# A decoder block: cross-attention's division moves to VectorE's block transposes, three norms share a tile, and the work is put in a new order

## The chip, the cores and the metric

The kernel runs on one core of a Trainium2 chip. The metric is the device time of one execution in microseconds, lower is better. Engines are named as in the profile: PE is TensorE's matrix products, PEld its weight loads, DVE is VectorE, ACT is ScalarE, POOL is GpSimd, SP is SyncE, which only issues transfers here.

## What is computed

One pre-norm decoder block in float32 on `x` of 32 sequences, 128 tokens, 256 features, with a context of the same shape:

```python
x = x + linear_attention(layernorm(x))     # 16 heads of 16; q, k = elu(.)+1; causal by cumulative sums;
                                           # num / (den + 1e-6), then an output projection; biases
x = x + cross_attention(layernorm(x), ctx) # 16 heads of 16; softmax(q k / 4) v; no biases, no projection
x = x + ffn(layernorm(x))                  # silu(x W1 s1) * (x W2 s2), gelu(. H1 s), gelu(. H2 s), . W3 s
```

The feed-forward width is 1024 and its weights are ternary with a scale for each output. The kernel uses a cheaper product for them, which is exact only if the weights survive a cast; it therefore compares each loaded weight with its original ("tests" below) and has a full-precision branch for the case that one differs. The branch is not taken with these inputs.

## The kernel before

**Pairs and steps.** The attention works on 16 pairs of sequences. A pair goes first through the units whose names begin with `a_` (self-attention), and three steps later (`SKEW`) through the `b_` units (cross-attention). A step `m` gives the engines the `a_` units of pairs near `m` and the `b_` units of pairs near `m - 3`. Each unit is a generator, cut by `yield` into parts; a part mostly holds the instructions of one engine. The lists `head`, `first0` to `first2`, `both`, `close`, `begins`, `alone`, `last` and `rest` are the order, written out: each entry advances one unit by one part. `both` is used for the steps 3 to 14, the steady ones; `close` is step 15, `begins` step 16, `alone` 17, `last` 18, `rest` 19. Inside an engine, instructions run strictly in this order.

**Self-attention of a pair.** `a_norm` takes statistics on VectorE (`pair_stats`, lines 129 to 151) and an inverse square root by three Newton rounds, on GpSimd from the third pair on, then GpSimd writes the normed rows. `a_transpose` turns them on TensorE, ScalarE copies. `a_keys`, `a_queries`, `a_values` project (`pp`, `pv`, lines 364, 372). `a_scores` puts all heads of one sequence into two double banks of PSUM (`sa`), and VectorE multiplies by the causal mask into `at` (line 488), for which there is one buffer per half. `a_weighted` multiplies with the values and a column of ones that gives the denominators (`pf`, line 409), in a layout with features on partitions. VectorE then transposes 32 by 32 blocks out of PSUM (`fa`, line 505), adds a constant and takes reciprocals, GpSimd multiplies (`oa`), VectorE transposes back (`oT`, line 517). `a_out` projects (`pw`) and VectorE adds to `x` (line 525).

**Cross-attention of a pair.** `b_norm`, `b_transpose`, `b_queries`, `b_keys`, `b_values` are alike. `b_maxima` computes scores once (`sm`) for their row maxima: two reductions on VectorE (line 581) and two small operations; `b_turn_maxima` transposes them (`pz`) and VectorE spreads them (`mT`, line 594). `b_scores` computes scores again (`se`) and adds the negative maxima by one more product (line 606), ScalarE takes exponentials (line 617). `b_weighted` is the same product `pf`, which ScalarE copies (`fb`, line 624). `b_divide` makes four transposes of 128 by 128 on TensorE (`po`, line 630), VectorE takes reciprocals and divides (lines 634, 636), GpSimd adds to `x` (line 643). `b_end` takes the norm of the finished pair for the feed-forward part.

**Buffers.** `sa`, `sm` and `se` share two double banks; every other product takes one of four banks in turn. So a product waits until the reader of the product four before it is done, and scores wait until the scores before them have been read.

**Tests.** `w_test` loads one slice of the weights W1, W2, H1 per step on GpSimd's queue, loads it again in two pieces on SyncE's, and VectorE compares (line 124). The slices of H2 and W3 are loaded and tested in the feed-forward part, in `layer`, two slices per layer from the second block on, until there are none left.

**Feed-forward part.** Eight blocks of four sequences, each value as a high and a low part: GpSimd casts the high one, VectorE subtracts for the low one, and TensorE multiplies both (`ph`, line 220). `beside` and `settle` in the last steps put the first block's input, gates and first products among the last cross-attention units; their low parts are on GpSimd.

The weights of the attention are permuted on the host (`by_group`) to fit the order of heads in `pf`.

## Time and profile before

| | us |
|---|---|
| median of 3 runs | 1106.37 |
| all runs | 1106.37, 1106.64, 1102.03 |
| the profiled execution | 1102.84 |
| its span in the trace | 1101.0 |
| granted TensorE clock, mean | 0.998 of full speed |

The profile's page has the busy time of each engine, the span in 40 slices of 27.5 us with the busy tenths of each engine, the chain that ended last, and groups of instructions: line, engine, operation, output and inputs, count, then busy time and mean ns of one, then the idle time just before them and what ended it. In the order of time, each line is a start, a length, an engine, a line and an operation; a bracket at its end is idle time before it and the releaser. The chain that ended last is 94% TensorE.

### The profile page before, as it was taken

The page shows a single profiled execution, that of the slowest core. Times are in us where ns is not written, and L with a number is a line of the kernel's source. Part 1 is how long each engine was busy: PE and PEld are TensorE (multiplying, and loading weights), DVE is VectorE, ACT ScalarE, POOL GpSimd, SP SyncE. Part 2 cuts the span into 40 slices and gives each one's busy share as a digit, 9 for nine tenths or more (in the row PEclk, how much of TensorE's full clock was granted, in tenths as well). Part 3 has the DMA queues.
Part 4 walks back from the last instruction along what each step waited for, and adds up shares of the span by engine and source line. Part 5 has one row for each costly group of instructions (what it writes and reads, how often), then busy time and mean ns, then how long its engine had stood idle before and what let it go on. Part 6 is the DMA issues. An engine that isn't in the chain of part 4 may idle for free.

```text
span 1101.0 us, 19995 instructions
## 1 busy us (share of the span) xinstructions
PE 1081.7 (98%) x8054; PEld 877.7 (80%) x8054; DVE 601.1 (55%) x1328; ACT 383.4 (35%) x591; POOL 453.3 (41%) x1057
## 2 busy tenths in 40 slices
PE   8989999999999999999999999999999999999997
PEld 6767777777777767688888888888888888888886
DVE  6889999999899876522532533422422422422412
ACT  4234444444444458831311312322312322312221
POOL 4656666666666455561411412312312312312311
PEclk9999999999999999999999999999999999999999
DMA  8001111111111100060110110000000000000000
GB/s 283 1 28 52 49 49 49 61 58 49 50 49 50 30 11 1 2 191 1 39 39 20 39 39 25 24 10 10 20 10 15 6 1 17 4 1 20 1 1 22
DMA packets 26546, 39.25 MB, mean 36 GB/s; under 512 B 2512, under 2 KB 18640, under 8 KB 26448
## 3 DMA queue, kind: packets, MB, share of 16 engines
q1 hardware_dynamic: 22000, 26.09, 7.0%
q0 software_dynamic: 4032, 11.54, 3.3%
q8 instruction: 65, 1.06, 0.4%
q10 hardware_dynamic: 416, 0.28, 0.1%
q14 instruction: 33, 0.27, 0.1%
HBM read 33.71 MB, written 4.19 MB: 34 GB/s over the span
## 4 chain that ended last, share of the span: by engine, by line
PE 94%; DVE 2%; ACT 1%; POOL 1%; issue 0%; DMA 0%; SPq 0%; DVEq 0%
PE ph L220 52%; PE pp L364 10%; PE py L864 6%; PE pf L409 5%; PE pv L372 5%; PE sa L393 3%; PE se L393 3%; PE sm L393 3%; PE pw L372 3%; PE po L630 1%; PE pt L353 1%; PE se L606 1%; DVE nm L581 1%; PE pt L209 1%; DVE at L488 1%; PE pz L591 1%
## 5 line engine op out<-in xcount | busy, mean ns | idle before, releaser
L183 DVE TENSOR_TENSOR gl<-hg,gh 128x512 fp32r<-128x512 f32 x126 | 87.6, 695 | 344.1 <-POOL gh L182 341.2
L182 POOL CAST gh<-hg 128x512 fp32r<-128x512 f32 x128 | 79.1, 618 | 358.9 <-ACT hg L244 358.9
L244 ACT ACTIVATE hg<-ph,col 128x512 f32<-128x512 f32 x128 | 88.3, 690 | 364.7 <-PE ph L220 364.6
L220 PE MATMUL ph<-sl,H 128*128 128x512 f32 x512 | 199.3, 389 | 0.5 <-POOL sl L183 0.5
L220 PE MATMUL ph<-sh,H 128*128 128x512 f32 x512 | 199.5, 390 | 0.0
L220 PE MATMUL ph<-gh,H 128*128 128x512 f32 x512 | 199.2, 389 | 0.0
L220 PE MATMUL ph<-gl,H 128*128 128x512 f32 x512 | 199.2, 389 | 0.0
L220 PEld LDWEIGHTS ph<-sl,H 128*128 128x128 f32 x512 | 96.1, 188 | 20.8 <-POOL sl L183 0.9
L220 PEld LDWEIGHTS ph<-sh,H 128*128 128x128 f32 x512 | 96.1, 188 | 20.4 <-issue 0.3
L220 PEld LDWEIGHTS ph<-gl,H 128*128 128x128 f32 x512 | 96.1, 188 | 20.0
L220 PEld LDWEIGHTS ph<-gh,H 128*128 128x128 f32 x512 | 96.1, 188 | 19.9
L220 PE MATMUL ph<-xh,W 128*128 128x512 f32 x256 | 101.4, 396 | 0.1
L220 PE MATMUL ph<-xl,W 128*128 128x512 f32 x256 | 100.7, 393 | 0.2 <-DVE xl L183 0.2
L182 POOL CAST sh<-hs 128x512 fp32r<-128x512 f32 x64 | 58.5, 915 | 71.8 <-DVE hs L236 71.7
L581 DVE TENSOR_REDUCE nm<-sm 128x8 f32<-128x1024 f32 x64 | 75.2, 1215 | 17.9 <-PE sm L393 17.9
L488 DVE TENSOR_TENSOR at<-sa,causal 128x1024 f32<-128x1024 f32 x64 | 75.2, 1216 | 8.7 <-PE sa L393 5.5
L617 ACT ACTIVATE pr<-se 128x1024 f32<-128x1024 f32 x64 | 62.0, 1020 | 27.6 <-PE se L606 27.6
L236 DVE SCALAR_TENSOR_TENSOR hs<-ph,col,sil 128x512 f32<-128x512 f32 x64 | 48.0, 750 | 41.9 <-PE ph L220 22.4
L234 ACT ACTIVATE sil<-ph,col 128x512 f32<-128x512 f32 x64 | 44.1, 690 | 75.8 <-PE ph L220 75.7
L364 PE MATMUL pp<-xTa,WA 128*128 128x256 f32 x256 | 62.1, 386 | 0.7 <-ACT xTa L356 0.7
L864 PE MATMUL py<-W,gh 128*128 128x256 f32 x256 | 62.7, 285 | 0.0
L864 PE MATMUL py<-W,gl 128*128 128x256 f32 x256 | 62.0, 283 | 0.0
(129 smaller groups left out, 1834.6 us busy)
## 6 DMA issues: line engine op xcount, KB each, us to landing
x<-in_x_dram SPq DMA_DIRECT2D x16, 256.0 KB, 5.5
cT<-in_ctxT_dram SPq DMA_DIRECT2D x16, 256.0 KB, 2.6
stage<-in_h1T_dram SPq DMA_DIRECT2D x16, 256.0 KB, 2.8
H<-in_h1T_dram POOLq DMA_DIRECT2D x8, 512.0 KB, 3.6
H<-in_h2T_dram POOLq DMA_DIRECT2D x8, 512.0 KB, 6.5
out_dram<-y SPq DMA_DIRECT2D x32, 128.0 KB, 1.7
raw<-in_h2T_dram SPq DMA_DIRECT2D x16, 256.0 KB, 2.6
WA<-in_wattn_dram SPq DMA_DIRECT2D x4, 256.0 KB, 4.8
```

Source lines behind the costliest of these rows:

```text
L182: (high_engine.copy if high_engine is nc.scalar else high_engine.tensor_copy)(high, t)
L183: lows.append(lambda: low_engine.tensor_tensor(low, t, high.bitcast(F32), ALU.subtract))
L220: nc.tensor.matmul(pp, lhsT=w[:, k, ts(c, P)], rhs=parts[p], start=(k == 0 and p == 0), stop=(k == len(src) - 1 and p == 1),)
L244: nc.scalar.activation(t, pp, AF.Gelu, scale=col[:, c_scale + c : c_scale + c + 1])
L364: nc.tensor.matmul(pp[:, c, :], lhsT=w[:, d, ts(c, P)], rhs=src[:, d, :], start=(d == 0), stop=(d == DC - 1))
L372: nc.tensor.matmul(pp, lhsT=src[:, d, :], rhs=w[:, d, :], start=(d == 0), stop=(d == DC - 1))
L393: nc.tensor.matmul(sc[g // 2][:, g % 2, 2 * c : 2 * c + 2, :], lhsT=loaded[32 * g : 32 * g + 32, c, ts(j, S)], rhs=streamed[32 * g : 32 * ...
L409: nc.tensor.matmul(pf[32 * g : 32 * g + 32, i, :], lhsT=v[:, 4 * i + g, :], rhs=weights[g // 2][:, g % 2, i, :], start=True, stop=True,)
L488: nc.vector.tensor_tensor(at.rearrange("p g i s -> p (g i) s"), sc[u].rearrange("p g i s -> p (g i) s"), causal.unsqueeze(1).to_broadcast( ...
L581: nc.vector.tensor_reduce(nm[:, 2 * u : 2 * u + 2, :], sc[u], AX.X, ALU.max, negate=True)
L617: nc.scalar.activation(pr, sc[u], AF.Exp)
L864: nc.tensor.matmul(py[:, :D], lhsT=h[k][p][:, ts(j, S)], rhs=W3[:, k, :], start=(k == 0 and p == 0), stop=(k == HC - 1 and p == 1),)
```

## The change

- `a_weighted`'s way from `pf` to divided values is made a function, `divided`, which `b_weighted` now uses too, without the added constant. `b_divide` goes; `b_out` turns the divided values by two transposes of 128 by 128 on TensorE (`pot`), ScalarE copies 256 columns, GpSimd adds to `x`.
- `pf` is filled with the heads in another order, so that the permutation on the host goes.
- `norms(k)` takes the statistics of three pairs (for self-attention `k + 2`, for cross-attention `k - 1`, for the feed-forward part `k - 4`) into one tile, and makes one round of small operations and one Newton iteration on six columns. Only the first two pairs of self-attention have a norm of their own, on VectorE, where a fused operation takes the place of two.
- `w_load` loads the slices of W1, W2 and H1 at the same rate as before but does not test them. `layer` tests all 28 slices, two per layer, from the first block's second layer to the last block's first.
- The lists have a new order. In a steady step TensorE's units were `sm pf pp sa po pp pp pz pf se mT pv pw pf sm pt po pv sa pz pp pt se mT pf pw`; they become `pt sm pt pv pot sa pz pp pw se mT pp sm pf pf sa pz pp pp se mT pv pf pf pot pw`.

```diff
+    means = tiny.tile([P, STEPS, 6], F32, name="means")
+    devs = tiny.tile([P, STEPS, 6], F32, name="devs")
...
+    def deviations(mv, nmean, rstd, engine=nc.gpsimd):
+        wide = [P, mv.shape[1]]
         nc.vector.tensor_scalar(nmean, mv[:, :, 0], -1.0, None, ALU.mult)
...
         for _ in range(NEWTON):
             engine.tensor_tensor(t, rstd, rstd, ALU.mult)
             engine.tensor_tensor(t, t, hv, ALU.mult)
-            engine.tensor_scalar(t, t, 1.5, None, ALU.add)
-            engine.tensor_tensor(rstd, rstd, t, ALU.mult)
+            if engine is nc.vector:
+                engine.scalar_tensor_tensor(rstd, t, 1.5, rstd, ALU.add, ALU.mult)
+            else:
+                engine.tensor_scalar(t, t, 1.5, None, ALU.add)
+                engine.tensor_tensor(rstd, rstd, t, ALU.mult)
...
-                        lhsT=v[:, 4 * i + g, :],
+                        lhsT=v[:, 8 * (i // 2) + 2 * g + i % 2, :],
...
+        def divided(pf, add, tags):
+            f = buffer([P, 4, S], F32, tag=tags[0], name=tags[0], bufs=2 if add else 1)
+            nc.vector.transpose(f.rearrange("p i s -> p (i s)"), pf.rearrange("p i s -> p (i s)"))
+            f = f.rearrange("p i (b w) -> p b i w", w=VW)
+            rden = small.tile([P, 4, 4], F32, tag="rden", name="rden", bufs=2)
+            if add:
+                nc.vector.tensor_scalar(rden, f[:, :, :, HD], add, None, ALU.add)
+                nc.vector.reciprocal(rden, rden)
+            else:
+                nc.vector.reciprocal(rden, f[:, :, :, HD])
+            yield
+            o = buffer([P, 4, 4, HD], F32, tag=tags[1], name=tags[1], bufs=2 if add else 1)
+            nc.gpsimd.tensor_tensor(
+                o, f[:, :, :, 0:HD], rden.unsqueeze(3).to_broadcast([P, 4, 4, HD]), ALU.mult
             )
+            yield
+            oT = buffer([P, DC, S], F32, tag=tags[2], name=tags[2], bufs=2 if add else 1)
+            nc.vector.transpose(
+                oT.rearrange("p c (b q) -> p b c q", q=32), o.rearrange("p b (c e) d -> p b c (e d)", e=2)
+            )
+            return oT
...
+        def norms(k):
+            a, b, e = ((n, 0 <= n < NPAIR) for n in (k + 2, k - 1, k - SKEW - 1))
+            mv = small.tile([P, 6, 2], F32, tag="mv", name="mv", bufs=2)
+            for c, (n, there) in enumerate((a, b, e)):
+                if there:
+                    pair_stats(mv[:, 2 * c : 2 * c + 2], n)
+                if c < 2:
+                    yield
+            of = [c for c, (_, there) in enumerate((a, b, e)) if there]
+            cols = slice(2 * of[0], 2 * of[-1] + 2)
+            yield from deviations(mv[:, cols], means[:, k, cols], devs[:, k, cols])
+            for c, (n, there) in enumerate((a, b)):
+                yield
+                if there:
+                    scal = means[:, k, 2 * c : 2 * c + 2], devs[:, k, 2 * c : 2 * c + 2]
+                    (A, Bs)[c][n]["xn"] = normed_pair(n, *scal, ("xna", "xnb")[c])
...
         def b_weighted(m, j):
             pf = weighted(Bs[m].pop(("w", j)), Bs[m]["v"][:, j])
             yield
-            f = buffer([P, 4, S], F32, tag="fb", name="fb")
-            nc.scalar.copy(f, pf)
-            Bs[m]["f", j] = f
-
-        def b_divide(m, j):
-            f, po = Bs[m].pop(("f", j)), bank("po")
-            for i in range(4):
-                nc.tensor.transpose(po[:, i, :], f[:, i, :], ident)
...
+            Bs[m]["oT", j] = yield from divided(pf, None, ("fb", "ob", "oTb"))
+
+        def b_out(m, j):
+            pt = bank("pot").rearrange("p a s -> p (a s)")[:, : DC * S]
+            oT = Bs[m].pop(("oT", j))
+            for c in range(DC):
+                nc.tensor.transpose(pt[:, ts(c, P)], oT[:, c, :], ident)
+            yield
+            o = buffer([P, D], F32, tag="oc", name="oc", bufs=1)
+            nc.scalar.copy(o, pt)
             yield
             nc.gpsimd.tensor_tensor(xs[m][:, j, :], xs[m][:, j, :], o, ALU.add)
...
-        def w_test(m):
-            if m < prologue or not spare:
-                return
-            n = spare.pop(0)
-            dst = (W1, W2, H1)[FFN_SLICES[n][0]]
-            load(n, dst)
-            pieces = again(lambda: stages.tile([P, TB], F32, tag="stage", name="stage"), n)
-            yield
-            test(dst, *pieces)
+        def w_load(m):
+            if m >= prologue and spare:
+                n = spare.pop(0)
+                load(n, (W1, W2, H1)[FFN_SLICES[n][0]])
+            return
+            yield
...
         both = [
...
+            (a_out, -1, 1), (b_scores, 0, 0), (b_queries, 1), (b_maxima, 0, 1), (norms, 0),
+            (b_weighted, 0, 0), (b_out, -1, 1), (b_queries, 1), (norms, 0), (b_maxima, 0, 1),
+            (a_keys, 1), (b_load, 2), (a_weighted, 0, 0), (a_scores, 0, 1), (b_turn_maxima, 0, 1),
+            (a_bias, 1), (norms, 0), (norms, 0), (b_weighted, 0, 0), (a_scores, 0, 1),
...
         rest = [
...
+            (b_weighted, -1, 1), (b_weighted, -1, 1), (norms, 0), (b_weighted, -1, 1), (norms, 0),
+            (b_weighted, -1, 1), settle, (b_out, -1, 1), (b_out, -1, 1), beside, (b_out, -1, 1), settle,
+            (norms, 0), (norms, 0), (norms, 0), (norms, 0),
...
-        loading, testing = iter(late), iter(late)
+        loading, testing = iter(late), iter(range(len(FFN_SLICES)))
...
-                if blk and c % 4 == 0:
+                if (blk or w is H2) and c % 4 == 0:
                     n = next(testing, None)
-                    waiting = None if n is None else (last_weights(n), *again(raw, n))
+                    waiting = None if n is None else (weights(n), *again(raw, n))
```

## The prediction

> **What bounds the kernel now.** I read the page first, for the busy shares and the forty slices, then the windows by stage, the order of time on TensorE, the waits and the groups.
>
> ```profile
> PE 1081.7 (98%) x8054; PEld 877.7 (80%) x8054; DVE 601.1 (55%) x1328; ACT 383.4 (35%) x591; POOL 453.3 (41%) x1057
> PE   8989999999999999999999999999999999999997
> DVE  6889999999899876522532533422422422422412
> ```
>
> TensorE is full nearly throughout; VectorE is nearly as full, but only in the first 400 us, the attention. The windows separate the stages:
>
> ```profile
> 0.00:50.00 50.00, 44.08 (x364) 34.61 (x364) 39.45 (x111) 16.94 (x38) 28.03 (x78) 1.00 0.46 156
> 100.00:150.00 50.00, 50.00 (x588) 38.67 (x584) 45.76 (x111) 22.26 (x40) 32.82 (x96) 1.00 0.17 54
> 400.00:450.00 50.00, 48.38 (x441) 35.26 (x433) 30.27 (x66) 39.77 (x52) 28.23 (x71) 0.97 0.00 1
> 800.00:900.00 100.00, 100.00 (x477) 84.25 (x476) 32.28 (x59) 23.99 (x34) 23.47 (x33) 1.00 0.03 9
> ```
>
> Columns: stretch, length, busy time of PE, PEld, DVE, ACT, POOL, granted clock, DMA. In the steady steps TensorE has no gap and VectorE works 46 of 50 us; in the feed-forward part VectorE works a third of the time. So a TensorE microsecond saved counts in full, and a VectorE microsecond counts only where its order makes TensorE wait. In the order of time the step repeats every 26.14 us (scores for the maxima start at 73.34, 99.48, 125.62). A piece of one step, and three waits of TensorE outside the steady steps:
>
> ```profile
> 99.41 1.15 PE L393 MATMUL sm<-kb,qb 32*128 32x256 f32 x16
> 103.42 1.15 PE L393 MATMUL sa<-qa,ka 32*128 32x256 f32 x16
> 104.49 0.66 PE L630 MATMUL po<-ident,fb 128*128 128x128 f32 x4
> ...
> 55.92 0.41 PE L409 MATMUL pf<-at,va 128*32 128x128 f32 x4 [1.41 <-DVE at L488]
> ...
> 61.75 1.13 PE L372 MATMUL pw<-WA,oT 128*128 128x256 f32 x4 [1.80 <-DVE oT L517]
> ...
> 468.02 0.66 PE L630 MATMUL po<-ident,fb 128*128 128x128 f32 x4 [0.71 <-ACT fb L624]
> ```
>
> **TensorE in a steady step.** I price a unit by the distance from its start to the next start, since busy times overlap: a projection 1.73, scores 1.07, weighting `pf` 1.01, four transposes 0.44 to 0.50, values 1.73, output projection `pw` 0.86, the `mT` addition 0.52 after 0.78 of scores, and about 0.2 more when an untiled product is followed by a tiled one. Two `po` per step (0.50 and 0.44) become two `pot` of half as many transposes (0.22 and, before scores, about 0.37): 0.35 less. The new order has six tiled runs per step, as before, but weighting and scores alternate in two places instead of four; the new sequence (names of the tiles) is pt 0.53, sm 1.08, pt 0.49, pv 1.73, pot 0.37, sa 1.08, pz 0.16, pp 1.73, pw 0.95, se 0.78, mT 0.52, pp 1.93, sm 1.07, pf 1.01, pf 1.01, sa 1.08, pz 0.16, pp 1.73, pp 1.93, se 0.78, mT 0.52, pv 1.84, pf 1.01, pf 1.01, pot 0.22, pw 0.86: 25.58 us, 0.56 less than 26.14.
>
> Against it stands one new wait. Between the second maxima scores and the next causal scores there were 4.01 us (99.41 to 103.42); the new order puts only two weightings there, 3.09. The two reductions start 1.18 after the scores and take 2.36, so the second half of the banks is free at 3.54 and wanted at 3.36: 0.2 to 0.3 us per step. The other places fit: causal scores after the first maxima come at 3.6, the output transposes of `pot` find their bank free with about 0.2 to spare (keys' three ScalarE copies, 1.75, just end), and values find theirs with 0.5. Taken: 25.58 + 0.25 = 25.83, 0.3 less, over 11 full steps 3.3 us. Bounds: 0.56 a step if the wait is hidden (6.2 us), and plus 0.5 a step if VectorE is 0.8 late (loss 5.5).
>
> **VectorE, ScalarE, GpSimd in the step.** Per batch, VectorE loses the divide (0.29 + 0.34 start to start, line 634, 636) and gains a transpose from PSUM with its reciprocal and one of 256 columns:
>
> ```profile
> L505 DVE STREAM_TRANSPOSE fa<-pf 128x512 f32<-128x512 f32 x32 | 22.8, 713 | 7.7 <-PE pf L409 6.6
> L517 DVE STREAM_TRANSPOSE oT<-oa 128x256 f32<-128x256 f32 x32 | 14.0, 437 | 0.5 <-POOL oa L512 0.5
> L624 ACT COPY fb<-pf 128x512 f32<-128x512 f32 x32 | 18.7, 584 | 50.4 <-PE pf L409 50.4
> L630 PE MATMUL po<-ident,fb 128*128 128x128 f32 x128 | 20.1, 279 | 0.8 <-ACT fb L624 0.7
> ```
>
> That is 0.95 + 0.36 - 0.63 = 0.7 more, 1.4 per step. Three norms in one tile save two of three groups of small operations, 1.0 per step; the moved tests (line 124, two of 0.69 and the reads) save 1.3. VectorE falls from 23.8 to about 23 of 25.8. GpSimd gains two products of 0.65 and loses 24 of 36 Newton operations at 0.28 start to start: 5.4 less. ScalarE copies 256 columns for 512. All are off the path, covered by TensorE. What is queued behind the one risky place: the norm statistics (3.5) and the four small operations (0.5) stand on VectorE directly before the second maxima; laid end to end behind the causal mask they finish at 12.52 where the scores are ready at 12.53. No margin: each 0.1 us of lateness is 0.1 per step.
>
> The Trainium skill speaks against the new transposes: "VectorE: DVE Perf Modes", Rules for kernel authors, gives a 128 by 128 transpose to TensorE when the result may lie in PSUM, and the VectorE one only 32 by 32 blocks; by it nothing would be taken off TensorE and this term would be zero. The trace already has block transposes at 713 and 437 ns with a weighting layout that makes the blocks suffice, on the engine that is not the bound, so the rows decide.
>
> **The prologue.** TensorE's waits between 16 and 62.8 us add up to 2.04 + 0.49 + 0.18 + 0.35 + 0.27 + 1.41 + 0.63 + 1.80 = 7.17. The last three come from two weightings in a row that share the one buffer of masked scores, and an output projection right behind. The new order puts the scores, the cross queries and the next queries between those weightings. Laid out with the rows' durations, the first 2.04 stays (the chain of keys through ScalarE and VectorE is the same), and some 0.3, 0.55, 0.6, 0.1 and 0.5 remain or arise in the first two steps: 4.1 in all, with steady steps beginning near 59. Newton with a fused add and multiply spares three VectorE operations of 0.2 in the first norm, at most 0.4 of the 0.68 wait at 10.1. Taken: 3.5 saved; bounds 4.7 (the most the layout gives) and 0 (new waits as long as the old).
>
> **The end of attention (376 to 472 us).** Ten `po` fewer by half: 2.2 saved. Before, the feed-forward input's transposes wait on GpSimd for 1.2 us in four pieces at 403 to 405 and the low part's split follows at once; between 406 and 412 the granted clock reads 0.80, 0.50 and 0.84 in stretches of 2 us, 1.7 us of work lost. In the new order scores, keys, maxima and transposes stand between that input and the first gates. I count 2 of these 2.9 as saved. Against that: for the last batch the weighting is followed at once by `pot`, with VectorE transpose and reciprocal (1.0), GpSimd product (0.65), VectorE transpose (0.45) and their hand-overs in between, 2.4 us where 0.71 stood: 1.7 lost. A transpose put before the `mT` product in the last steps, and close's causal mask between two scores with 2.3 us where 3.5 are needed, cost about 1.3 together. Sum: 1.2 saved; bounds 5 saved, 3 lost. On the clock, "TensorE: Matmul & The Clock Gate", Part 1, ties the half rate to an idle window of about 3.4 us; the trace halves it after four gaps below 0.6, and keeps 1.00 through the 2.04 gap at 16.7, so the page decides nothing here.
>
> **The feed-forward part.** 24 tests (24 of 0.69 + 0.08, 18.5 us of VectorE) move here; two pieces per four chunks behind the low part, on an engine a third busy, while TensorE runs 14.8 us of products per four chunks. Their loads go through SyncE's queue behind the outputs of the block before, and their tiles are the ones the gates have freed. Cost taken 0; if a gate had to wait for a test, 1.5 us in each of six blocks more, 9 at the worst. The weights' own loads stay on GpSimd, 0.6 each. In the attention SyncE's queue loses the tests' 24 loads; the context loads left in it wait for TensorE to free their buffer, so that brings nothing.
>
> **Sum.** 3.3 + 3.5 + 1.2 = 8.0 off the profiled execution's 1102.84 (span 1101.0): 1094.8. The runs before were 1102.03, 1106.37 and 1106.64, so the profiled one is low by up to 3.8; I put the forecast at half of that above the sum, 1096.5.
>
> **Rivals.** (1) *The saved TensorE time is spent at new waits*: the 0.25 per step is 0.55, the prologue gives 1.5 and the end nothing; 1.5 to 3 saved, about 1100.5 to 1103. For it: VectorE's missing margin; against it: VectorE's load falls. (2) *Slower: VectorE's in-order queue decides the step.* If statistics that wait for GpSimd's sum (cross-attention's last result, now behind a copy) start over 0.55 late, the maxima reductions behind them slip, the causal scores with them, and the saving of 0.56 is used up. At 1.4 late in each of 12 steps: 0.85 x 12 = 10 lost, less 3.5 + 1.2 elsewhere, 5.5 slower, about 1108 to 1112. The sum they wait for is done some 6 us earlier by the layout, which speaks against it. (3) *More than counted*: the 0.25 is hidden and the prologue gives 4.7, the end 2: 12.9 saved, 1090 to 1092. (4) That the change doesn't do what it says: the transposes' end is modelled, and halving them may free nothing; then 0.35 of each step is missing, which is rival 1.
>
> **Chances.** Forecast 0.60, rival 1 with 4 0.20, rival 2 0.10, rival 3 0.10. A measurement of this kernel can tell about 0.5%, 5.5 us, from no change. The forecast's own spread leaves 0.08 of its 0.60 within that; with rival 3, faster is 0.62, within 0.28, slower 0.10. The range 1089 to 1104 takes in the forecast's bounds, rival 3 and most of rival 1; rival 2 is left out.
>
> **What would show it.** Right: steps of 25.7 to 26.0 us; about 0.2 us waits of causal scores on the maxima reduction (line 608 after); steady steps from 58 to 60; full clock around 400; feed-forward stretches still at 100.00. Wrong: steps of 26.1 or longer, waits of tiled scores above 0.5, TensorE gaps in the feed-forward part that end with a test.

## The result and the profile after

The changed kernel takes 1097.41 us (median of six runs, 1096.79 to 1098.78) against 1105.33 for the kernel before (six runs, 1102.03 to 1106.64): ratio 0.9934, 95% interval 0.9918 to 0.995. The profiled execution took 1097.11, its span is 1095.1, so 5.9 less than the span of 1101.0 before. The forecast was 1096.5.

The page first: busy times of the engines, and two rows of the 40 slices.

```profile
PE 1079.6 (99%) x7990; PEld 877.8 (80%) x7990; DVE 610.5 (56%) x1250; ACT 374.8 (34%) x591; POOL 413.8 (38%) x777
PE   8999999999999999899999999999999999999997
DVE  5888888888888877623433433433433432423412
```

TensorE has 64 products fewer; it is still the full engine. VectorE is busier by 9 us in all, GpSimd 40 us less busy. The windows of the changed kernel, with the columns as before:

```profile
0.00:50.00 50.00, 44.82 (x357) 35.09 (x358) 35.59 (x98) 16.34 (x37) 26.39 (x67) 0.97 0.43 146
100.00:150.00 50.00, 50.00 (x552) 38.48 (x547) 44.27 (x93) 22.86 (x42) 25.88 (x56) 1.00 0.12 33
400.00:450.00 50.00, 48.78 (x480) 35.84 (x478) 33.94 (x68) 45.07 (x58) 27.90 (x54) 1.00 0.02 7
800.00:900.00 100.00, 100.00 (x477) 84.33 (x476) 37.03 (x71) 23.65 (x33) 23.67 (x33) 1.00 0.09 30
```

The clock is 0.97 in the first window (it was 1.00) and 1.00 around 400 (it was 0.97). VectorE's tests show in the last row, 37 us for 32, beside a TensorE that has no gap. In the order of time on TensorE a steady step now looks so, from the first to the second causal scores and on to the next second maxima:

```profile
90.28 1.15 PE L402 MATMUL sa<-qa,ka 32*128 32x256 f32 x16
91.36 0.33 PE L618 MATMUL pz<-ident,z 128*128 128x128 f32 x1
...
97.44 1.30 PE L402 MATMUL sm<-kb,qb 32*128 32x256 f32 x16
98.67 1.08 PE L418 MATMUL pf<-pr,vb 128*32 128x128 f32 x32
99.57 1.06 PE L418 MATMUL pf<-at,va 128*32 128x128 f32 x32
100.55 1.83 PE L402 MATMUL sa<-qa,ka 32*128 32x256 f32 x16
102.31 0.33 PE L618 MATMUL pz<-ident,z 128*128 128x128 f32 x1
...
123.58 1.30 PE L402 MATMUL sm<-kb,qb 32*128 32x256 f32 x16
```

From 97.44 to 123.58 is 26.14 us, to the hundredth what a step took before. The same 16 products of causal scores take 1.08 to the next start at 90.28, and 1.76 at 100.55. No bracket on these lines shows the wait, because it lies inside the group. The weight loads (PEld) of the same products show it: the first four are loaded, then the engine stands 0.40 until a maxima reduction (`nm`) is done, then come the other twelve.

```profile
100.55 0.30 PEld L402 LDWEIGHTS sa<-qa,ka 32*128 32x128 f32 x4 [0.20 <-issue]
101.25 0.73 PEld L402 LDWEIGHTS sa<-qa,ka 32*128 32x128 f32 x12 [0.40 <-DVE nm L608]
```

On VectorE at that place:

```profile
98.25 0.18 DVE L150 TENSOR_SCALAR devs<-v 128x6 int32<-128x6 int32 x1
98.35 0.60 DVE L152 TENSOR_SCALAR hv<-v 128x6 f32<-128x6 f32 x1
98.85 2.34 DVE L608 TENSOR_REDUCE nm<-sm 128x8 f32<-128x1024 f32 x2
```

The reductions that free the banks start 1.41 after their scores, where they start 1.18 after them when VectorE is free (112.81 to 113.99 in the same step), and they end at 101.19.

So where did 5.9 us go? The first steady product (`pt` now, `sm` before) starts at 60.14 instead of 62.81: 2.7 saved. The scores for the maxima of step 15 start at 373.56 instead of 376.11: 2.55, so the twelve steady steps gave nothing. The last turn of cross-attention starts at 462.07 instead of 468.02: 5.95, so the end of attention gave 3.4. From there to the end it is 633.0 in both. The end of attention and its waits, in the order of time:

```profile
375.06 0.41 PE L657 MATMUL pot<-ident,oTb 128*128 128x128 f32 x2 [0.35 <-DVE oTb L450]
391.50 0.92 PE L402 MATMUL se<-qb,kb 32*128 32x256 f32 x10 [0.16 <-DVE at L541]
442.77 0.33 PE L618 MATMUL pz<-ident,z 128*128 128x128 f32 x1 [1.03 <-DVE hs L245]
462.07 0.44 PE L657 MATMUL pot<-ident,oTb 128*128 128x128 f32 x2 [2.30 <-DVE oTb L450]
```

These are 3.8 us of waits, against 3.5 before in other places. What the stage saved is busy time of TensorE, 88.16 to 84.49 in the windows between the two marks. Of that, 1.7 is what a lowered clock had taken at 406 to 412. Run 1 below, which gives each turn four transposes again, is only 0.73 longer in this stage (378.24 to 467.48), so the halved turns are worth 0.7 here. About 1 us of the 3.4 is not assigned to a cause.

### The profile page after: what moved, and what is told of

It reads as the page before. It is cut to its first block, busy times and chain, and to the rows that moved or that the text cites. A ratio compares the mean times of both kernels' runs of the same rounds, so it can differ in the third digit from the quotient of the medians.

```text
span 1095.1 us, 19472 instructions
## 1 busy us (share of the span) xinstructions
PE 1079.6 (99%) x7990; PEld 877.8 (80%) x7990; DVE 610.5 (56%) x1250; ACT 374.8 (34%) x591; POOL 413.8 (38%) x777
## 4 chain that ended last, share of the span: by engine, by line
PE 94%; DVE 3%; POOL 2%; issue 1%; ACT 0%; POOLq 0%; DVEq 0%
PE ph L229 52%; PE pp L373 10%; PE py L882 6%; PE pf L418 5%; PE pv L381 5%; PE sa L402 4%; PE sm L402 3%; PE se L402 3%; PE pw L381 2%; PE pt L362 1%; DVE at L541 1%; PE pot L657 1%; PE se L633 1%; PE pz L618 1%; PE pt L218 1%
## 5 line engine op out<-in xcount | busy, mean ns | idle before, releaser
L500 ACT ACTIVATE e<-pp,col 128x256 f32<-128x256 f32 x64 | 26.8, 470 | 127.4 <-PE pp L373 96.7
```

## The experiments

I held four questions open. Do the halved turns count in full? What sets the step at 26.14: the second causal scores' wait (A), or VectorE's load (B)? What did the tests and the order bring? And where does the lowered clock come from, which stood at 406 us in the trace before and stands at 20 us now? Ratios are to the kernel before.

**1. Four turns instead of two.** `b_out` makes the two transposes twice, the second pair beside the first and unread.

```diff
...
-            for c in range(DC):
-                nc.tensor.transpose(pt[:, ts(c, P)], oT[:, c, :], ident)
+            for c in range(2 * DC):
+                nc.tensor.transpose(pt[:, ts(c, P)], oT[:, c % DC, :], ident)
...
```

> The kernel after, with the two transposes of the divided values made twice on TensorE (the second pair is written beside the first and never read), so that TensorE again makes four per batch. Theory A (TensorE's sequence sets the step, plus one wait of the causal scores for the second maxima reduction, 0.68 us a step of which 0.23 is VectorE being late): two transposes of 0.11 more per batch, 0.44 a step; part of it, up to 0.23, can be taken up by that lateness, so 3.5 to 7 us longer in all. Rival B (VectorE's total work sets the 26.14 us step and TensorE's savings are swallowed): under 1 us longer. Rival C (no wait, TensorE's new sequence simply costs 26.14): 7 us longer.

1103.53, ratio 0.9996 (0.9982 to 1.001): no faster than the kernel before. The step is 26.58, 0.44 longer, and the second causal scores keep their 1.83: in the steps nothing is absorbed. The halved turns are worth some 6 us (1103.53 less 1097.41; in the trace 12 steps of 0.44 and the 0.7 at the end of attention). Without them the rest of the change has no net effect that is clear of noise. Rival B, which foretold under 1 us, is out.

**2. Less of the maxima.** The second sequence's maxima are taken over 32 of 128 keys.

```diff
-  nm[:, 2 * u : 2 * u + 2, :], sc[u], AX.X, ALU.max, negate=True
+  nm[:, 2 * u : 2 * u + 2, :], sc[u][:, :, :, : 32 if j else S], AX.X, ALU.max, negate=True
```

> The kernel after, with the maxima of the second sequence of each pair reduced over 32 of the 128 keys only (the other three quarters of that reduction are left out), so that the two reductions take about 0.7 us instead of 2.36. Theory A: the causal scores no longer wait, a steady step falls from 26.14 to 25.4 to 25.6, 12 steps give 6.5 to 9 us less, about 1089. Rival B: VectorE has 1.6 us less per step, so the step falls by as much until TensorE is full, the same 25.4 to 25.6 or less; the wait itself tells nothing. Rival C: no change, since nothing waits.

1088.87, ratio 0.9877 (0.985 to 0.9903). On TensorE, the second scores of a step and the next step's mark:

```profile
96.53 1.30 PE L402 MATMUL sm<-kb,qb 32*128 32x256 f32 x16
99.64 1.15 PE L402 MATMUL sa<-qa,ka 32*128 32x256 f32 x16
...
121.99 1.30 PE L402 MATMUL sm<-kb,qb 32*128 32x256 f32 x16
```

The step is 25.46. VectorE lost some 1.6 a step, but the step only 0.68, exactly the excess of the second scores. 25.46 is thus what TensorE's sequence takes without that wait, as A foretold. But B foretold the same step, so this run rules out only that nothing waits; runs 1 and 8 speak against B.

**3. The waiting turn filled.** In `rest`, `beside` is moved ahead of the last `b_out`.

```diff
-            (b_weighted, -1, 1), settle, (b_out, -1, 1), (b_out, -1, 1), beside, (b_out, -1, 1), settle,
+            (b_weighted, -1, 1), settle, beside, (b_out, -1, 1), (b_out, -1, 1), (b_out, -1, 1), settle,
```

> The kernel after, with the last piece of feed-forward work in the last step put before the last batch's output transposes instead of behind them. Theory A: TensorE's wait of 2.30 us before those transposes is filled with 3.7 us of products, 2.0 to 2.3 us less, about 1095. Rival: the wait comes back behind them, because the first layer's later products wait for the values of the piece moved or the last norm is late; no change.

1097.65, ratio 0.9947 (0.9931 to 0.9963). The edit moved no product on TensorE, and the turn waits 2.30 as before: all chunks of the feed-forward part that are worked in beside the attention have been given by then, and this `beside` is empty. The question stayed untested here; run 6 asks it again.

**4. Second scores later by order.** A projection is put ahead of them, and with it several units of the second half of the step move.

```diff
-            (a_keys, 1), (b_load, 2), (a_weighted, 0, 0), (a_scores, 0, 1), (b_turn_maxima, 0, 1),
+            (a_keys, 1), (b_load, 2), (a_weighted, 0, 0), (a_queries, 1), (a_scores, 0, 1),
...
-            (a_queries, 1), (b_weighted, 0, 0), (b_keys, 1), (b_scores, 0, 1), (a_values, 1),
+            (a_queries, 1), (b_weighted, 0, 0), (b_keys, 1), (a_values, 1), (b_keys, 1),
...
+            (b_scores, 0, 1), (a_weighted, 0, 0), (a_values, 1), (b_out, 0, 0), (a_out, 0, 0),
+            (a_weighted, 0, 1), (a_out, 0, 0), (a_weighted, 0, 1), (a_weighted, 0, 1),
+            (b_weighted, 0, 1), (b_weighted, 0, 1), (b_out, 0, 0), (b_weighted, 0, 1), (b_out, 0, 0),
```

> The kernel after with another order of the second half of the steady step: queries before the causal scores, values before the cross scores, the cross weighting after the output projection. Theory A: the causal scores start 1.9 us later and find their banks free, 0.68 less per step, one more tiled run 0.2 more: steps of 25.6 to 25.8, 4 to 6 us less in all. Rival B: VectorE's total sets the step, 26.1 again, no change within 1 us. Rival C: no wait to remove and one more border, 2.4 us longer.

1101.46, ratio 0.9976 (0.9964 to 0.9988): slower than the changed kernel, and none of the three expectations. Both causal scores of one step, and what stands on VectorE before the first maxima:

```profile
89.72 1.73 PE L402 MATMUL sa<-qa,ka 32*128 32x256 f32 x16
...
102.49 1.15 PE L402 MATMUL sa<-qa,ka 32*128 32x256 f32 x16
```

```profile
87.57 0.45 DVE L450 STREAM_TRANSPOSE oTb<-ob 128x256 f32<-128x256 f32 x1 [0.80 <-POOL ob L445]
87.94 2.31 DVE L608 TENSOR_REDUCE nm<-sm 128x8 f32<-128x1024 f32 x2
```

The second scores run freely, but now the first ones stop, since the first maxima are late: they start 1.83 after their scores (86.11), where 1.18 would do. VectorE was not short of time there. It stood 0.80 for GpSimd's product, because the cross weighting that feeds it had moved to the end of the step. The wait went to the other reduction; the step is 26.34.

**5. Statistics behind the scores.** `norms`' third part (1.7 us of VectorE) is put behind the causal mask, and its Newton steps after that.

```diff
-            (b_weighted, 0, 0), (b_out, -1, 1), (b_queries, 1), (norms, 0), (b_maxima, 0, 1),
+            (b_weighted, 0, 0), (b_out, -1, 1), (b_queries, 1), (b_maxima, 0, 1),
...
-            (a_bias, 1), (norms, 0), (norms, 0), (b_weighted, 0, 0), (a_scores, 0, 1),
-            (b_turn_maxima, 0, 1), (a_weighted, 0, 0), (b_weighted, 0, 0), (a_queries, 1),
-            (a_queries, 1), (b_weighted, 0, 0), (b_keys, 1), (b_scores, 0, 1), (a_values, 1),
+            (a_bias, 1), (b_weighted, 0, 0), (a_scores, 0, 1),
+            (b_turn_maxima, 0, 1), (norms, 0), (a_weighted, 0, 0), (b_weighted, 0, 0), (a_queries, 1),
+            (a_queries, 1), (b_weighted, 0, 0), (norms, 0), (norms, 0), (b_keys, 1), (b_scores, 0, 1), (a_values, 1),
```

> Nothing is left out: in the steady steps the third pair's statistics and the four small operations on the shared tile (1.7 us of VectorE) move from before the second maxima reductions to behind the causal mask that follows them. A (the second causal scores wait because the reductions start 0.23 us after their scores are there, and then the rest of a group that has been stopped costs 1.06): the reductions start at once, the distance from those scores to the next product falls from 1.76 to about 1.5, the step from 26.14 to 25.9, 12 steps: 2.5 to 3 us less than the changed kernel, near 1094.7. B (VectorE has no room left: what is taken from one place makes it late at the next, as in the run with the other order): the 1.7 us come back behind the causal mask, at the next scores or at the next step's transposes, and the step stays at 26.1 or grows; 1097 to 1101.

1146.97, ratio 1.0395 (1.0375 to 1.0415), far outside both expectations. The small step that A foretold is there: the second scores go from 1.76 to 1.54. But a turn then waits 3.08 us, by this chain (GpSimd, VectorE, TensorE, in the order of time):

```profile
112.95 0.62 POOL L445 TENSOR_TENSOR oa<-fa,rden 128x256 f32<-128x256 f32 x1
```

```profile
113.60 0.45 DVE L450 STREAM_TRANSPOSE oT<-oa 128x256 f32<-128x256 f32 x1 [3.66 <-POOL oa L445]
113.97 0.65 DVE L526 TENSOR_TENSOR va<-pv,row 128x512 f32<-128x512 f32 x1
```

```profile
114.68 0.69 PE L657 MATMUL pot<-ident,oTb 128*128 128x128 f32 x2 [3.08 <-DVE va L526]
```

GpSimd's twelve Newton operations (107.96 to 111.8) and the two writes of normed rows behind them now stand ahead of self-attention's product; VectorE stands at the transpose that needs it, and the addition that frees a bank stands behind that. A step takes about 30.6 us, the clock being lowered behind the gap as well. This is a mechanism of the kind of the prediction's rival 2, VectorE's in-order queue standing still for GpSimd, though at another place than rival 2 named: 50 us more than the changed kernel, for 1.7 us of VectorE work put in the wrong place.

**6. The last chunk in two halves.** Eight of the last chunk's sixteen products go ahead of the last weighting, eight behind it.

```diff
...
+            pp = hidden(w, src, c, None, 0)
+            yield
+            hidden(w, src, c, pp, 1)
...
-            (b_weighted, -1, 1), (b_weighted, -1, 1), (norms, 0), (b_weighted, -1, 1), (norms, 0),
+            (b_weighted, -1, 1), more, (b_weighted, -1, 1), (norms, 0), (b_weighted, -1, 1), (norms, 0),
```

> Nothing is left out: the sixteen products of the last feed-forward chunk that is worked in beside the attention are given as eight before and eight behind the last weighting. A (the 2.30 us wait before the last turn is VectorE, GpSimd and VectorE in a row with nothing for TensorE to do, and eight products of 0.23 fit in it): the wait falls to 0.3 to 0.5, the weighting itself may wait up to 0.5 on its exponentials, 1.3 to 1.8 us less from there on, near 1095.9. B (what ends last there is not this chain but ScalarE's exponentials and the statistics behind it): the turn moves with the weighting and less than 0.5 is saved.

1096.25, ratio 0.9934 (0.9917 to 0.995). That is the ratio of the changed kernel, so what the edit brought is read from the trace alone. The turn starts at 461.47 instead of 462.07, 0.6 earlier:

```profile
461.47 0.44 PE L664 MATMUL pot<-ident,oTb 128*128 128x128 f32 x2 [1.03 <-DVE oTb L457]
```

Between A and B. The weighting came 1.8 earlier, but ran 0.4 longer (it stopped for its exponentials), and GpSimd was still in its Newton steps and an addition to `x` until 460.3, when the divide's product could begin. That row is what ends last there.

**7. Idle transposes in the first gap.**

```diff
         give(head, 0)
+        again_idle = scores_banks("idle")[0]
+        for n in range(16):
+            nc.tensor.transpose(again_idle[:, 0, n % 4, :], ident, ident)
```

> Sixteen transposes of the identity, written to a bank that nobody reads, fill the 2.04 us in which TensorE waits for the first keys at 16.9 us; they add nothing to the result. A (the halved clock at 20 to 24 us, about 1.7 us of lost work, follows from this gap): the granted clock stays at 1.00 through 18 to 26, and everything behind comes 1.5 to 1.7 us earlier, near 1095.8. B (the lowered clock belongs to the time since the start or to something else and only falls where it falls): the clock still reads about 0.5 to 0.7 there, time within 0.5 us of the changed kernel.

1097.3, ratio 0.9942 (0.9925 to 0.9958). Two windows of the changed kernel, and the same two of this run (length, busy PE, PEld, DVE, ACT, POOL, clock):

```profile
20.00:22.00 2.00, 2.00 (x9) 1.64 (x6) 1.84 (x2) 0.00 (x0) 0.00 (x0) 0.57 1.05 371
22.00:24.00 2.00, 2.00 (x12) 1.20 (x14) 0.90 (x5) 0.44 (x2) 0.81 (x4) 0.58 0.21 71
```

```profile
20.00:22.00 2.00, 2.00 (x12) 1.37 (x10) 2.00 (x2) 0.36 (x1) 0.00 (x0) 1.00 1.02 359
22.00:24.00 2.00, 2.00 (x44) 1.45 (x44) 0.51 (x5) 1.21 (x4) 1.03 (x6) 1.00 0.17 57
```

In the profiled execution the clock stays at 1.00, the steady steps begin at 58.78, 1.4 earlier, and the time is 1095.8, as A foretold. Of the 1.4, 0.4 was there by the first transposes (`pt`, 9.33 instead of 9.72), so the lowered stretch had cost 1.0. But the other three runs have a mean clock of 0.997, as the changed kernel has, where the profiled one has 0.999, and took 1097.3 to 1098.1; their traces were not taken, and the median is that of the changed kernel, as B foretold. One profile does not decide: run 8 below keeps the gap and has no stretch there either. Run 11 brings more.

**8. The tests back in the attention.** `w_test` as before takes the place of `w_load`; its comparison stands in the second half of the step, and the feed-forward part tests only the slices of H2 and W3 again.

```diff
-            (a_weighted, 0, 0), (a_values, 1), (a_weighted, 0, 1), (b_weighted, 0, 1),
+            (a_weighted, 0, 0), (w_test, 0), (a_values, 1), (a_weighted, 0, 1), (b_weighted, 0, 1),
```

> The tests of the first weights (two pieces of 0.69 us a step on VectorE, their reads on SyncE's queue) go back into the attention, at a place where VectorE has about 1.4 us of idle time spread over four gaps; the other order, the shared tile and the halved turns stay. A (only what stands directly before a late reduction counts): the gaps take nearly all of it, the step grows by 0 to 0.3, 0 to 4 us more, 1097.5 to 1101.5, and the feed-forward part stays at 633. B (VectorE's total sets the step): 1.4 a step, 17 us more, near 1114.

1096.43, ratio 0.9931 (0.9914 to 0.9947); the step is 26.15. Two comparisons a step more on VectorE cost nothing, because they stand where VectorE had gaps. A, or slightly better: the moved tests brought nothing, and B is out, which foretold 17 us more. This run also shows another place for the lowered stretch. With the 2.04 gap at 16.9 as it was, its clock is 1.00 at 20 to 24, and instead:

```profile
460.00:462.00 2.00, 1.49 (x7) 1.30 (x8) 0.94 (x3) 0.94 (x2) 1.92 (x3) 0.92 0.00 0
462.00:464.00 2.00, 2.00 (x6) 1.51 (x6) 1.08 (x6) 0.72 (x1) 0.77 (x2) 0.50 0.00 0
464.00:466.00 2.00, 2.00 (x8) 1.59 (x7) 0.00 (x0) 0.00 (x0) 1.42 (x8) 0.72 0.00 0
```

That is right behind the other gap of over 2 us, the last turn's 2.30. Eight other profiles have this gap (the changed kernel, runs 1 to 5, 7 and 9), and none of them has a stretch behind it.

**9. Two small operations on GpSimd.**

```diff
-        nc.vector.tensor_scalar(nmean, mv[:, :, 0], -1.0, None, ALU.mult)
...
-        nc.vector.tensor_scalar(hv, v, -0.5, None, ALU.mult)
         yield
+        engine.tensor_scalar(hv, v, -0.5, None, ALU.mult)
+        engine.tensor_scalar(nmean, mv[:, :, 0], -1.0, None, ALU.mult)
```

> Nothing is left out: two of the four small operations that stand on VectorE directly before the second maxima reductions (the negated means and the halved variances, 0.08 and 0.6 us start to start) are made on GpSimd ahead of its Newton steps. A (lateness of the reductions counts one to one): the reductions start when their scores are there, 0.23 us earlier; the distance from the second causal scores to the next product falls from 1.76 to 1.53, as it did in the run with the statistics moved; step 25.9, 11 steps: 2.5 us less than the changed kernel, near 1094.9. B (GpSimd's row of Newton steps is already what the next step waits for, as the run with the statistics moved showed with its 3 us waits): the two operations, some 0.6 us, come back there; step 26.1 or longer, 1097 to 1103.

1095.64, ratio 0.9924 (0.9907 to 0.9942). VectorE's reductions and TensorE's scores in a step:

```profile
98.17 2.36 DVE L608 TENSOR_REDUCE nm<-sm 128x8 f32<-128x1024 f32 x2 [0.28 <-PE sm L402]
```

```profile
96.99 1.29 PE L402 MATMUL sm<-kb,qb 32*128 32x256 f32 x16
100.10 1.61 PE L402 MATMUL sa<-qa,ka 32*128 32x256 f32 x16
101.64 0.33 PE L618 MATMUL pz<-ident,z 128*128 128x128 f32 x1
```

The reductions wait for their scores and start 1.18 after them; the excess is 0.46 instead of 0.68, and the step 25.92, 0.22 less: A to the hundredth. The time fell 1.8 and not 2.5. In the profiled execution the steady steps begin at 59.60 with the clock at 1.00 all the way, against 58.78 in run 7, but that is not the edit: the difference is there by the first transposes (10.13 against 9.33), and run 12, which has the same edit, has them at 9.23. What the median lacks stays open.

**10. The divide alone, in the old order.** The kernel before, with `divided`'s steps for cross-attention, and the order of heads that they need, put into its lists by hand.

```diff
-            f = buffer([P, 4, S], F32, tag="fb", name="fb")
-            nc.scalar.copy(f, pf)
+            f = buffer([P, 4, S], F32, tag="fb", name="fb", bufs=1)
+            nc.vector.transpose(f.rearrange("p i s -> p (i s)"), pf.rearrange("p i s -> p (i s)"))
...
-            (b_maxima, 0, 0), (b_maxima, 0, 0), (b_transpose, 1), (a_queries, 0), (a_norm, 1),
+            (b_maxima, 0, 0), (b_weighted, -1, 1), (b_maxima, 0, 0), (b_transpose, 1), (a_queries, 0), (a_norm, 1),
```

> The kernel before with only the divide of cross-attention put on VectorE square transposes; the old order stays but for where the divide's own steps stand; tests, norms and the rest as before. A (halving the turns pays in the measure in which TensorE need not wait for the longer chain of VectorE, GpSimd, VectorE, and the old order, with 1.4 us more on VectorE per step and no operations taken from it, has no room for that): new waits before the turns or the causal scores of 0.5 to 2 a step, step 26.3 to 28, 1105 to 1125. B (the turns count wherever they stand): the step falls by 0.35 to 25.8, near 1099.

1179.91, ratio 1.0692 (1.0663 to 1.0722); a step takes about 31 us. Both expectations were far off, A too, which had steps of 26.3 to 28. In every steady step the first turn waits:

```profile
96.55 0.44 PE L644 MATMUL pot<-ident,oTb 128*128 128x128 f32 x2 [2.59 <-DVE oTb L635]
```

VectorE comes to this chain late (norm operations and the comparisons stand ahead of it), and in nearly every step the clock is lowered behind the gap (a step without that takes 29.49). So B is out: the halved turns do not count wherever they stand. That the old order has no room for the longer chain is shown for this placing only; how well another hand could place it is left open.

**11. Three edits together**, those of runs 6, 7 and 9.

> Nothing is left out: the two small operations on GpSimd, the sixteen idle transposes in the first gap and the last feed-forward chunk in two halves, together. A (each edit takes away another wait, and a lowered clock of about 1.7 us of lost work follows only where TensorE waited): 2.5 from the steps, 0.6 from the last turn, 1.7 from the clock, since no gap over 1.1 us is left: 1097.4 less 4.8, near 1092.6, with the clock at 1.00 from 10 to 1080 us. B (the lowered clock comes once a run wherever it may, and the small operations come back on GpSimd): 0.6 to 1 us less, 1096.5.

1093.4, ratio 0.9904 (0.9887 to 0.9921), with the six runs between 1092.96 and 1094.37 and clocks of 0.998 to 0.999. The profiled clock reads 1.00 in every window of 2 us from 4 to 1088. A, 0.8 short of its number. A had taken 1.7 for the clock, but a stretch behind the first gap costs the prologue 1.0, as in run 7; with 1.0 the sum is 1093.3.

**12. Half a projection ahead of the second scores**, on top of run 11.

```diff
+        def a_half(m):
+            A[m]["pp"] = project(WQ, A[m]["xT"], chunks=[0])
...
-            (a_keys, 1), (b_load, 2), (a_weighted, 0, 0), (a_scores, 0, 1), (b_turn_maxima, 0, 1),
+            (a_keys, 1), (b_load, 2), (a_weighted, 0, 0), (a_half, 1), (a_scores, 0, 1), (b_turn_maxima, 0, 1),
```

> Nothing is left out: the three edits of the run before, and in the steady steps the first half (0.87 us) of the projection of the next queries stands between the two weightings and the second causal scores, its other half where the whole stood. A (what is left of the step's excess over 25.46 is the restart of scores that come 0.45 us before their bank is free): the second causal scores run without a stop (1.15 in the record, 1.08 to the next product), the step falls from 25.92 to 25.5 to 25.7 (a change between tiled and untiled products more), 11 steps: 2.5 to 5 us less than the run with three edits, 1088.5 to 1091. B (the wait goes to the other reduction, as in the run with the scores later): the first causal scores then wait 0.4 or more, the step stays at 25.9, near 1093.4.

1090.07, ratio 0.9872 (0.9853 to 0.989). Both causal scores of a step, with the half projection before the second:

```profile
88.66 1.15 PE L410 MATMUL sa<-qa,ka 32*128 32x256 f32 x16
...
98.93 1.13 PE L381 MATMUL pp<-xTa,WA 128*128 128x256 f32 x4
99.99 1.15 PE L410 MATMUL sa<-qa,ka 32*128 32x256 f32 x16
```

Neither stops, and the first maxima are not late either; the step is 25.66, 0.48 less than before the change, where the halved turns were counted at 0.35. This version leaves no work out and beats the changed kernel by 7.3 us and the kernel before by 14.9.

## Why the prediction was right, and where its steps were not

The time was met, and in part by luck, by terms that were off in both directions: the steady steps gave nothing of their 3.3, the end of attention 3.4 instead of 1.2, the prologue 2.7 of 3.5. The sum of 8.0 saved was 2.1 too much against the spans (5.9), and the 1.7 that was added to the base made up for most of it. By the prediction's own signs the steps went wrong: a step of 26.1 or longer and waits of tiled scores above 0.5 stood there as signs of being wrong, and both came (26.14 and 0.68). The full clock around 400 and the full feed-forward stretches came as signs of being right; steady steps from 58 to 60 were just missed, at 60.14.

- **The sequence of a steady step**, 25.58: right to 0.12. Run 2 shows 25.46 once nothing waits. (The starts named for the maxima scores before, 73.34, 99.48 and 125.62, stand in the trace at 73.27, 99.41 and 125.55; the distance of 26.14 is right.) The turns in it, counted at 0.35, are worth 0.44 (run 1).
- **The new wait**, 0.25 a step: this is the step that failed; it measured 0.68. The place, the cause and the lack of margin were named. Three things make the size: 0.18 between 3.36 and 3.54, as laid out; 0.22 because the reductions came late, for which the two small operations `means` and `hv` are enough (run 9 takes them away; `hv` alone took 0.44 more than elsewhere); and the rest, about 0.3, because four of the sixteen products run before the stop, yet the twelve behind it take 1.12 from the bank's release to the next start and not three quarters of 1.08. A bank that is 0.4 late costs 0.7. Run 9 agrees: with the reductions in time the excess is 0.46, which is 0.18 and 0.28. What the restart spends its 0.3 on is not shown.
- **VectorE's load against its order.** Rival 1's condition came true for the steps (more than 0.55 a step), in part because VectorE's queue was late, as in rival 2 but small. Runs 2, 4, 5 and 8 show that VectorE's total does not decide here: 1.6 us less gave 0.68, 1.4 us more cost 0.01, and the same work in another order cost 0.2 or 4.5 a step.
- **The prologue.** The waits fell from 7.17 to 3.0, where 4.1 had been laid out to remain, and the steady steps begin at 60.14 where 59 was foretold. 1.0 of the difference is the clock, 0.57 and 0.58 at 20 to 24 us, which the prediction had left at 1.00 behind the first gap because the trace before did. Another 0.5 is the start: the first transposes stand at 9.72, in the trace before at 9.26. From there to the steady steps it was 53.55, is 50.42 now, and is 49.45 in run 7 without the stretch; the term was rather too small.
- **The end of attention.** The last turn's wait (1.6, where 1.7 was counted) was right. The turns were counted at 2.2, and run 1 shows 0.7. The clock around 406 came back in full, 1.7; that the new order did this was not tested. The 1.3 us of other costs did not add to those before: the waits of the stage are 3.8 against 3.5.
- **The feed-forward part**, 0: right, 633.0 in both, with 37 us of VectorE in 100 instead of 32.
- **The moved tests** were counted as room for VectorE; run 8 shows that they brought nothing.
- **The base.** Half of the spread of the runs before was to be added for a low profiled execution (half of 3.8 is 1.9; 1.7 was added). Those runs differ by clock: in the comparisons made with the experiments, runs of the kernel before with a mean clock of 0.999 took 1100.7 and 1101.7, those with 0.995 took 1104.8 to 1106.3. The six runs of the changed kernel have 0.997, one of them 0.998. The changed kernel's profiled execution was not low (1097.11 against a median of 1097.41), so the 1.7 added for a low one helped the number by luck. One lowered stretch takes 1.7 us of TensorE's work, 0.0015 of the mean clock in 1100 us. The medians differ by 7.9 us and the profiled spans by 5.9; the 2 us between these figures are of the size of one such stretch, an estimate and not traced.

## What to carry to other kernels

An engine that is nine tenths busy and off the critical path is not priced by its total but by what stands directly before the result that somebody waits for: move one 0.5 us operation from there before moving 1.4 us from elsewhere. When an order is written out by hand, follow each shifted unit through every queue that it joins; statistics and Newton steps put a few places later cost 50 us through GpSimd. Look inside groups of products for waits: a record of 1.83 for 1.15 is a wait, though no bracket of the products shows it; the weight loads of the same products do. Half a unit of independent work put before it took it away (run 12), where a whole one, with other units moved along, only moved it (run 4).

## What the hardware showed

- **A lowered clock behind gaps of 2 to 3 us.** It reads 0.5 for some 3.4 us and takes 1.7 us of TensorE's work, which is not always 1.7 us of time. From the first transposes to the steady steps, the six profiles that have the stretch there (the changed kernel, runs 1 to 4 and 6) take 50.42 to 50.49 and the six that have not (runs 5, 7, 8, 9, 11 and 12) 49.45 to 49.48: 1.0 us. The 2.04 gap near 16.9 stands in eleven profiles (both kernels, runs 1 to 6 and 8 to 10); seven of them have the lowered stretch between 18 and 26, and four have not (the kernel before, runs 5, 8 and 9). With that gap filled (runs 7, 11 and 12) three profiles of three have none. Behind run 5's 3.08 and run 10's 2.59 it comes in nearly every step. With no gap above 1.2 us (runs 11 and 12) there is none while TensorE works, and all ten executions of these two runs have a mean clock of 0.998 or more, against five of the 24 of the changed kernel and runs 6 to 9. So the gaps are very likely the cause; that is a count and not a trace of each execution. The Trainium skill's "TensorE: Matmul & The Clock Gate", Part 1, describes a free-running window of about 3.4 us; a stretch of this length, and a gap that may bring it or not, agree with that. Its rule under "Why this matters for your kernels", no gaps above about 3 us, is too wide here: a gap of 2.04 us was followed by the stretch in seven profiles of eleven. Why the stretch at 406 of the kernel before came behind four gaps below 0.6 us was not tried.
- **The start of an execution scatters by over 1 us.** The first transposes (`pt`) come between 9.03 (run 8) and 10.20 (run 3) in the fourteen profiles, while the granted clock reads 1.00 there. A difference of 1 us between two single profiles can be this alone, as with runs 7 and 9.
- **A small operation on VectorE at 0.60 instead of 0.16.** In the steady steps `hv` took 0.60 in all ten places, each time beside an operation of GpSimd on 512 columns (98.24 in the step shown). The six columns are not the cause: run 5 has the same operation at 0.16 to 0.17, begun while GpSimd was idle, and in the kernel before an operation on two columns took 0.58, in the eleven places where it began 0.06 behind a GpSimd product, and 0.17 in the others.

```profile
107.79 0.17 DVE L152 TENSOR_SCALAR hv<-v 128x6 f32<-128x6 f32 x1
```

```profile
112.07 0.58 DVE L137 TENSOR_SCALAR nmean<-mv 128x2 f32<-128x2 f32 x1
```

Other small operations beside GpSimd kept to 0.15 to 0.19, so what exactly lengthens these is not shown; taking the operation off VectorE was enough.
